# An attention block with Strassen products: v's last sums in place, its transpositions in pieces, and three orders on VectorE

## The chip, the core and the metric

The kernel runs on one core of a Trainium2 chip, as one program. A core has a TensorE (PE, matrix products out of SBUF into PSUM), a VectorE (DVE, element-wise work and transpositions of 32 x 32 blocks), a ScalarE (ACT, the exponential and copies), a GpSimd (POOL) and a SyncE (SP), which here mostly issue DMAs. Each engine takes its instructions in the order of its own queue and waits on semaphores for the others. The metric is the device time of the program in microseconds; lower is better.

## The reference

An input x of 16 images, 512 channels and 32 x 32 points goes through a group norm (8 groups), a product with a 1536 x 512 matrix that gives q, k and v, attention with 4 heads of 128 channels over the 1024 points, a product with a 512 x 512 matrix, and is added to the result. All in float32.

```python
xn = ((xg - mu) * rsqrt(var + EPS)).reshape(b, c, h, w) * gamma + beta
q, k, v = split(einsum('oc,bchw->bohw', qkv_w, xn) + qkv_b, 3, axis=1)   # to heads: b, 4, 1024, 128
attn = softmax(einsum('bhnd,bhmd->bhnm', q, k) * scale, axis=-1)
out = einsum('bhnm,bhmd->bhnd', attn, v)
return x + einsum('oc,bchw->bohw', proj_w, out) + proj_b
```

## The kernel before

**Attention.** The main loop (L2364) takes 16 images x 4 heads x 8 steps of 128 keys. A step has two halves of 512 queries: a product for the scores (`score`, L1704), an exponential on ScalarE into `p` (L1710), and one step later the product with v into `po` (L1801). The running sum `tot` of the exponentials is VectorE's (L1723, L1725). When a head is over, `denominators` transposes it (L1734), sums it and takes the reciprocal; DMAs spread it over the partitions as `rinv`, and `divide` (L1814) multiplies the head's output by it at step 4 of the next head.

**Products between.** Into each half of a step the loop puts one entry of a list `halfway`: a few TensorE units of the products for the next image (q, k, v) or the last one (the projection). So TensorE's order is scores, weighted sum, some units of Strassen products, scores and so on.

**Strassen products.** `strassen` (L623) makes a 2 x 2 block product from seven products p1 to p7, in the order 1, 2, 6, 5, 7, 4, 3, out of weights kept in DRAM and inner sums t1 to t4 of the moving blocks. p1, p6, p7 and p4 gather in a PSUM bank x, p5 and p3 in a bank y, of which there is one (`ps_z`, one buffer). A result c22 is VectorE's sum of bank y and ScalarE's copy of bank x after p7; p3 is written into bank y, so it waits for c22, and c12 is read from y after p3.

**Images 0 to 3** use `two_levels` (L699), a Strassen product of Strassen products: four groups g of inner products, whose results lie in tiles R[0] to R[2] (tags r0 to r2, turned by one from call to call; R[3] is R[0] again). `make_sum` makes the inner sums t1 to t4 of a group on VectorE (L757). `combine` queues the outer sums in `pending`, of which each unit runs one when it is over: `add` (L908) and `done`, which calls the caller's `finish` for the results c11, c22, c21, c12. For v, `finish` (L1056) adds two parts and v's bias into the first half of a tile `vt` of the pool `ypool` (two buffers, tag y), `turn_v` transposes it into the second half of that tile (L1068), GpSimd sends it to DRAM (`vd`, L1076) and reads it back in v's layout (L1087). What is still in `pending` at the end of v's last group goes to a list `late["tail"]`, of which the main loop runs two per half of a step (L2405), behind the step's other units. The products for v of the next image run in head 3, those for q and k of heads 0 and 1 in head 2, those for heads 2 and 3 in head 0 of that image.

**Images 4 to 15** use `thirds` (L1099): 15 outer products in 8 groups for each of two pairs of heads, G = 0 to 15, out of thirds of the columns. They run in heads 2 and 3 of the image before and in head 0, and the last units of G = 15 (p4, p3) in the first half of head 1. `out_` (L1268) evicts their results; L1287 is c22 (and c12) on VectorE. `turn_part` transposes v in 128 x 256 pieces (L1348).

**The projection** of the image before (`proj_groups`, L1645) is a `two_levels` with a `prepare` function and runs in head 1. Its first unit stands in the same half as the last units of the thirds. Its inner sums of group 0 are in the tile home_B, those of group 1 in a tile `pp_t`. The outer sums of its operand (`sums_of_b`, L415) are VectorE's too.

**Order.** A planner lays each engine's instructions in order before the program runs: by priority (by and large the order in which the program names them; `tc.high_priority` puts them ahead) and by when, by its estimate, their inputs are there. `with tc.issue_after(i)` puts the instructions of the block that are on i's engine behind i in that engine's queue. It can place an instruction well ahead of the step that names it. On the chip each queue is then followed as it stands.

Of the kernel before, what the change touches and what calls it, by code (L numbers as in the profile page):

```python
# [16 lines left out]
P = 128  # L17
# [214 lines left out]
def fast_path(ctx, tc, x, sources, out, consts, flag, dims):  # L232
# [466 lines left out]
    def two_levels(name, site, b, blocks, finish, sums="make", homes="BBBB", prepare=None):  # L699
# [11 lines left out]
        def placed():  # L711
            return tc.high_priority(URGENT) if opening else nullcontext()
# [28 lines left out]
        def make_sum(g, m):  # L741
            n = len(OUTER[g])
            to = sum_tile(g, m)
            a, c = {
                "t1": ("b12", "b11"), "t2": ("b22", "t1"), "t3": ("t2", "b11"),
                "t4": ("b21", "t2"),
            }[m]
            with ExitStack() as order:
                if sums == "keep" and g == 0 and m in ("t1", "t2"):


                    order.enter_context(tc.issue_after(added[b - 1, 1, NB - 1].ins))
                    order.enter_context(tc.high_priority(URGENT))
                if (b, site) == (0, 1) and (g > 0 or m in ("t3", "t4")):
                    order.enter_context(tc.issue_after(beside["scores"].ins))
                for i in range(n):
                    nc.vector.tensor_sub(  # L757
                        to[:, i, :], inner_block(g, i, a), inner_block(g, i, c)
                    )
            if sums == "keep":  # L760
                t = dpool.tile([P, n, Q], F32, tag=f"{m}_{g}", bufs=1, name=f"kept_{m}_{g}")
                inner_kept[b, g, m] = t
                nc.gpsimd.dma_start(t, to)

        def group_units(g):
# [99 lines left out]
            def end():  # L865
                combine(g)
                if g == len(OUTER) - 1:
                    if site == "v":
                        late["tail"] = late.get("tail", []) + pending
                    else:  # L870
                        with placed():
                            run(pending)
                    pending.clear()


# [47 lines left out]
        def combine(g):  # L923

            if g == 1 and opening:
# [9 lines left out]

                pending.extend((lambda: None, lower))
            elif g == 1:
                done("c11", (0, 0), (1, 0))
                add((1, 1), (0, 0), (1, 1))
                add((1, 0), (1, 1), (0, 1))  # L940
            elif g == 2 and opening:
                add((2, 0), (1, 1), (2, 0), 0)
# [109 lines left out]
    def v_groups(b):  # L1052
        rows = {}


        def finish(which, h, a, c):  # L1056
            pair, half = int(which[1]) - 1, int(which[2]) - 1
            two = ypool.tile([P, KC, HALF], F32, tag="y", name=f"vt_{b}_{pair}_{h}_{half}")
            t = two[:, 0]
            i = 2 * pair + h  # L1060
            nc.vector.scalar_tensor_tensor(t, a, vb_sb[:, i : i + 1], c, ALU.add, ALU.add)
            turn_v(b, pair, half, h, t, two[:, 1], rows)

        return two_levels(f"v_{b}", "v", b, lambda: xb[b], finish, "load", "ABAB")

    def turn_v(b, pair, half, h, t, u, rows):
        n = P // BLK
        nc.vector.transpose(  # L1068
            u.rearrange("p (q i j) -> p j q i", q=n, i=BLK),
            t.rearrange("p (j q i) -> p j q i", q=n, i=BLK),  # L1070
        )
        if h == 0:
            rows[half] = dpool.tile(
                [2 * P, HALF], F32, tag="v", name=f"vd_{b}_{pair}_{half}"
            )
        nc.gpsimd.dma_start(rows[half][ts(h, P), :], u)  # L1076
        if h == 1:
            read_v(b, pair, half, rows[half])
# [20 lines left out]
    def thirds(b):  # L1099
# [151 lines left out]
        def group_units(G):  # L1251
# [16 lines left out]
            def out_(which, a, c=None):  # L1268
# [14 lines left out]
                with tc.high_priority(URGENT):  # L1283
                    if c is None:
                        evict(dst, view(a), row, G)
                    else:
                        nc.vector.tensor_add(dst, view(a), view(c))  # L1287

            us = strassen(
                f"t_{b}_{G}", mm, out_, n * H3,  # L1290
# [49 lines left out]
        def turn_part(p, h, part):  # L1340
            half, q = divmod(part, 2)
            if (p, half) not in turned:
# [2 lines left out]
                ]  # L1345
            u = turned[p, half][0]
            n = P // BLK
            nc.vector.transpose(  # L1348
                u[:, h].rearrange("p (q i j) -> p j q i", q=n, i=BLK)[:, ds(2 * q, 2)],
                made["vt"][:, h, ts(part, Q)].rearrange("p (j q i) -> p j q i", q=n, i=BLK),  # L1350
            )
            turned[p, half][1] += 1
            if turned[p, half][1] < 2 * KC:
                return
# [374 lines left out]
    def denominators(b, h):  # L1729
# [1 line left out]
        t = tot.pop((b, h))  # L1731

        tt = lpool.tile([P, N // BLK, BLK], F32, tag="tt", name=f"tt_{b}_{h}")
        nc.vector.transpose(tt.rearrange("p c m -> p (c m)"), t)  # L1734
        part = lpool.tile([P, N // BLK], F32, tag="part", name=f"part_{b}_{h}")
        nc.vector.tensor_reduce(part, tt, AX.X, ALU.add)

# [626 lines left out]
    for s in range(steps + 1):  # L2364
# [15 lines left out]
        for half in range(NH2):  # L2380
            if s < steps:
                scores(s, half)
                if j in (2, 3) and half == 0 and s > NB:
                    with tc.issue_after(exps[s].ins):
                        spread_inverse(*where(s - NB)[:2], j - 2)
                if half == 1 and j == 4 and s > NB:

                    with tc.issue_after(added[b, h, 4].ins):
                        divide(*where(s - NB)[:2])
                if half == 1 and s in biased:  # L2390

                    with tc.issue_after(exps[s].ins):
                        bias_of_v(0, biased[s])
# [167 lines left out]
```

## Time and profile before

| | us |
|---|---|
| median of 3 runs | 3120.81 (3120.13 to 3120.99) |
| the profiled execution, its own time | 3120.64 |
| its span, first to last instruction | 3119.1 |
| ScalarE busy | 1727.8 |
| all DMA packets, mean rate | 204 GB/s |

The mean granted TensorE clock is 0.999. A timeline row reads: start in us from the first instruction, length in us, engine, line, operation, tiles written and read, shape, count of merged instructions and, in brackets, the idle time of the engine before it and what ended it. Idle times under 0.15 us aren't printed. A matmul's length has its way through the array in it, so that the next one starts before it ends: a hole is seen in the distance of two starts. A float32 product stands in the records as two matmuls, one behind the other.

In the timeline of TensorE, image 2 begins at 424.8 us, image 4 at 819 us, and from image 4 on each image takes 192.4 us.

### The profile page before, as it was taken

Reading aid. Unit: us, or ns where it says so; the run is one execution under the profiler, and the core shown is the slowest. Engines: PE = TensorE matmul, PEld = TensorE weight load, DVE = VectorE, ACT = ScalarE, POOL = GpSimd, SP = SyncE. Lnnn points to the kernel's source line nnn. Section 1 sums busy time; section 2 is a strip of 40 time slices with the busy share of each in tenths; the row PEclk is TensorE's granted clock in tenths of the full one; section 3 lists DMA queues with packets and bytes.
Section 4 is the critical chain, followed back from the end, with each engine's and each line's share of the span. In section 5 each row is a group of like instructions: output and inputs, shape, how many; then the busy total and the mean of one; then the engine's idle time right before and its main releaser. Section 6 shows DMA issues by size and latency. Waiting matters only on the chain. (4 is left out here: it accounts for less than half of the span.)

```text
span 3119.1 us, 38289 instructions
## 1 busy us (share of the span) xinstructions
PE 3105.8 (100%) x11934; PEld 2265.7 (73%) x11934; DVE 2692.3 (86%) x4604; ACT 1727.8 (55%) x3744; POOL 469.0 (15%) x792
## 2 busy tenths in 40 slices
PE   9999999999999999999999999999999999999999
PEld 7567766777777777777777777777777777777775
DVE  9988888789798897988979889798898988989787
ACT  3545536455465655656556565565655656556543
POOL 0131121111111111211112111111111111111010
PEclk9999999999999999999999999999999999999999
DMA  5576765666767667666676666766667676676651
GB/s 173 173 229 198 246 196 196 211 197 212 233 219 221 194 206 224 199 217 201 200 224 208 215 200 205 222 204 210 204 203 226 198 213 206 211 221 194 222 192 42
DMA packets 244064, 636.80 MB, mean 204 GB/s; under 512 B 32656, under 2 KB 77840, under 8 KB 243856
## 3 DMA queue, kind: packets, MB, share of 16 engines
q1 hardware_dynamic: 164912, 363.58, 38.3%
q0 software_dynamic: 66272, 236.38, 21.8%
q10 hardware_dynamic: 12672, 34.35, 3.5%
q8 instruction: 96, 1.57, 0.2%
q14 instruction: 112, 0.92, 0.1%
HBM read 462.49 MB, written 171.69 MB: 203 GB/s over the span
## 5 line engine op out<-in xcount | busy, mean ns | idle before, releaser
L1801 PE MATMUL po<-p,v 128*128 128x512 f32 x2048 | 1046.3, 593 | 0.0
L1704 PE MATMUL s<-qk,qk 128*128 128x512 f32 x2048 | 1045.6, 592 | 0.0
L1710 ACT ACTIVATE p<-s 128x512 f32<-128x512 f32 x1024 | 610.7, 596 | 520.2 <-PE s L1704 510.6
L1801 PEld LDWEIGHTS po<-p,v 128*128 128x128 f32 x2048 | 616.2, 301 | 375.9 <-issue 259.7
L1725 DVE TENSOR_TENSOR tot<-tot,p 128x1024 f32<-128x1024 f32 (+1 forms) x408 | 472.6, 1159 | 159.8 <-ACT p L1710 156.5
L1704 PEld LDWEIGHTS s<-qk,qk 128*128 128x128 f32 x2048 | 362.0, 189 | 52.3 <-issue 24.2
L1287 DVE TENSOR_TENSOR r<-t_y,t_u 128x342 f32<-128x342 f32 (+1 forms) x384 | 186.4, 485 | 138.6 <-PE t_y L1263 111.6
L1378 DVE TENSOR_TENSOR r<-r,r 128x684 f32<-128x684 f32 x264 | 226.4, 865 | 1.4
L1263 PE MATMUL t_x<-home_A,w 128*128 128x171 f32 x1008 | 187.8, 308 | 0.3 <-DVE home_A L1181 0.3
L1263 PE MATMUL t_x<-home_B,w 128*128 128x171 f32 x1008 | 187.7, 308 | 0.0
L1263 PEld LDWEIGHTS t_x<-home_A,w 128*128 128x128 f32 x1008 | 161.6, 189 | 30.8 <-issue 20.1
L1263 PEld LDWEIGHTS t_x<-home_B,w 128*128 128x128 f32 x1008 | 161.6, 189 | 30.2 <-issue 20.1
L1087 POOL DMA_DIRECT2D v<-vd x240 | 139.7, 589 | 156.5 <-DMA vd<-vu 54.3
L1150 DVE TENSOR_TENSOR f<-x 128x684 f32<-128x684 f32 x168 | 144.1, 858 | 0.8
L1223 ACT COPY t_u<-t_x 128x342 f32<-128x342 f32 x192 | 78.5, 409 | 119.6 <-PE t_x L1263 111.9
L293 POOL DMA_DIRECT2D x<-in_x x60 | 32.7, 548 | 645.2 <-PE t_x L1263 410.4
L1263 PEld LDWEIGHTS t_z<-f,w 128*128 128x128 f32 x528 | 89.5, 190 | 51.9 <-issue 34.4
L792 PE MATMUL pp_x<-home_B,w_proj 128*128 128x256 f32 x414 | 107.1, 379 | 0.0
L1348 DVE STREAM_TRANSPOSE vu<-vt 128x256 f32<-128x256 f32 x192 | 104.7, 647 | 0.0
L1229 ACT ACTIVATE t_u<-t_x,bias 128x171 f32<-128x171 f32 x192 | 72.1, 402 | 56.7 <-PE t_x L1263 56.6
L1263 PE MATMUL t_y<-f,w 128*128 128x171 f32 x528 | 101.3, 310 | 1.3 <-DVE r L1287 0.6
L1188 POOL DMA_DIRECT2D kept_t<-home_A x96 | 52.4, 546 | 321.5 <-DVE home_A L1181 312.1
(393 smaller groups left out, 5227.9 us busy)
## 6 DMA issues: line engine op xcount, KB each, us to landing
w<-kept SPq DMA_DIRECT2D x182, 512.0 KB, 3.9
w<-kept SPq DMA_DIRECT2D x182, 384.0 KB, 3.9
kept_t<-home_A POOLq DMA_DIRECT2D x96, 342.0 KB, 3.8
home_B<-kept_t SPq DMA_DIRECT2D x96, 342.0 KB, 3.3
rinv<-row ACTq DMA_DIRECT2D x63, 512.0 KB, 4.3
x<-in_x POOLq DMA_DIRECT2D x60, 512.0 KB, 5.7
v<-vd POOLq DMA_DIRECT2D x240, 128.0 KB, 4.3
out_y<-y_c POOLq DMA_DIRECT2D x60, 512.0 KB, 3.3
```

Of the source, the lines that this page charges most:

```text
L792: latest["product"] = nc.tensor.matmul(acc[:, ts(i, Q)], have["w"][t][:, i, slot, :], inner(i, bn), start=(first and i == 0), stop=True, s ...
L1087: nc.gpsimd.dma_start(vs[b, pair][ts(q, BLK), half].rearrange("m h (k i) j -> m (h k) (i j)", k=n), rows.rearrange("(k m) (q e) -> q m k e ...
L1150: (eng.tensor_add if op == "+" else eng.tensor_sub)(made[f], of(a), of(c))
L1223: nc.scalar.copy(dst, src)
L1263: latest["product"] = nc.tensor.matmul(acc[:, ts(i, H3)], wts[G, t][:, i, slot, :], moving, start=(start and i == 0), stop=True, skip_grou ...
L1287: nc.vector.tensor_add(dst, view(a), view(c))
L1348: nc.vector.transpose(u[:, h].rearrange("p (q i j) -> p j q i", q=n, i=BLK)[:, ds(2 * q, 2)], made["vt"][:, h, ts(part, Q)].rearrange("p ( ...
L1378: (nc.vector.tensor_add if add else nc.vector.tensor_sub)(at(o), a, c)
L1704: latest["score"] = nc.tensor.matmul(sc, ks[b, h][:, ts(j, P)], qs[b, h][:, ts(half, HALF)], start=True, stop=True)
L1710: exps[s] = nc.scalar.activation(ps[s][:, ts(half, HALF)], sc, AF.Exp, scale=SCALE)
L1725: added[b, h, j] = nc.vector.tensor_add(tot[b, h][:, i], tot[b, h][:, i], ps[s][:, i])
L1801: summed = nc.tensor.matmul(po[half], v_block(b, h, j), ps[s][:, i], start=(j == 0), stop=(j == NB - 1),)
```

## The change

- v's `finish` writes its sum over one of the two parts it adds (over c for c22, else over a), and takes one tile of the pool `ypool` for both heads of a result, for the transposed halves alone. Because c11's sum now overwrites R[0][:, 0], `combine` puts the addition that reads it ahead of c11's two sums when the site is v.
- At the end of v's last group what is left in `pending` is run there, as for the other sites, and not put into `late["tail"]`.
- `turn_v` and `turn_part` transpose in pieces of 128 columns: four instructions in place of one of 512, two in place of one of 256.
- In `thirds`, `late["third"]` holds the latest c22 eviction. The projection's inner sums of group 0, and t3 and t4 of group 1, are put behind it on VectorE, and so is the transposition of `tot` of each head 0.
- In head 0 of image 4 (`old`) `divide` comes at step 5, behind that step's running sum, and not at step 4.

```diff
@@ make_sum
+                if prepare and (g == 0 or (g, m) in ((1, "t3"), (1, "t4"))) and "third" in late:
+                    order.enter_context(tc.issue_after(late["third"].ins))
@@ end
                 if g == len(OUTER) - 1:
-                    if site == "v":
-                        late["tail"] = late.get("tail", []) + pending
-                    else:
-                        with placed():
-                            run(pending)
+                    with placed():
+                        run(pending)
                     pending.clear()
@@ combine
             elif g == 1:
+                if site == "v":
+                    add((1, 1), (0, 0), (1, 1))
                 done("c11", (0, 0), (1, 0))
-                add((1, 1), (0, 0), (1, 1))
+                if site != "v":
+                    add((1, 1), (0, 0), (1, 1))
                 add((1, 0), (1, 1), (0, 1))
@@ v_groups, finish
-            two = ypool.tile([P, KC, HALF], F32, tag="y", name=f"vt_{b}_{pair}_{h}_{half}")
-            t = two[:, 0]
+            if h == 0:
+                rows["to"] = ypool.tile(
+                    [P, KC, HALF], F32, tag="y", name=f"vt_{b}_{pair}_{half}"
+                )
+            t = c if which == "c22" else a
             i = 2 * pair + h
             nc.vector.scalar_tensor_tensor(t, a, vb_sb[:, i : i + 1], c, ALU.add, ALU.add)
-            turn_v(b, pair, half, h, t, two[:, 1], rows)
+            turn_v(b, pair, half, h, t, rows["to"][:, h], rows)
@@ turn_v
-        nc.vector.transpose(
-            u.rearrange("p (q i j) -> p j q i", q=n, i=BLK),
-            t.rearrange("p (j q i) -> p j q i", q=n, i=BLK),
-        )
+        to = u.rearrange("p (q i j) -> p j q i", q=n, i=BLK)
+        of = t.rearrange("p (j q i) -> p j q i", q=n, i=BLK)
+        for k in range(HALF // P):
+            nc.vector.transpose(to[:, k], of[:, k])
@@ thirds, out_
-                        nc.vector.tensor_add(dst, view(a), view(c))
+                        out = nc.vector.tensor_add(dst, view(a), view(c))
+                        if which == "c22":
+                            late["third"] = out
@@ turn_part
-            nc.vector.transpose(
-                u[:, h].rearrange("p (q i j) -> p j q i", q=n, i=BLK)[:, ds(2 * q, 2)],
-                made["vt"][:, h, ts(part, Q)].rearrange("p (j q i) -> p j q i", q=n, i=BLK),
-            )
+            to = u[:, h].rearrange("p (q i j) -> p j q i", q=n, i=BLK)[:, ds(2 * q, 2)]
+            of = made["vt"][:, h, ts(part, Q)].rearrange("p (j q i) -> p j q i", q=n, i=BLK)
+            for k in range(2):
+                nc.vector.transpose(to[:, k], of[:, k])
@@ denominators
-        nc.vector.transpose(tt.rearrange("p c m -> p (c m)"), t)
+        third = late.get("third") if h == 0 else None
+        with tc.issue_after(third.ins) if third is not None else nullcontext():
+            nc.vector.transpose(tt.rearrange("p c m -> p (c m)"), t)
@@ main loop
-                if half == 1 and j == 4 and s > NB:
+                if half == 1 and j == (5 if (b, h) == (old, 0) else 4) and s > NB:
-                    with tc.issue_after(added[b, h, 4].ins):
+                    with tc.issue_after(added[b, h, j].ins):
                         divide(*where(s - NB)[:2])
```

## The prediction

> **What bounds the kernel now.** I read the page first: its span and busy times.
>
> ```profile
> span 3119.1 us, 38289 instructions
> PE 3105.8 (100%) x11934; PEld 2265.7 (73%) x11934; DVE 2692.3 (86%) x4604; ACT 1727.8 (55%) x3744; POOL 469.0 (15%) x792
> ```
>
> TensorE is busy all the time but 13.3 us (3119.1 - 3105.8). The change neither adds nor removes a product, so it can only win what lies in the holes of PE, and in matmuls that run at a lower clock behind a hole. I therefore read PE's timeline around its holes and, in the same places, VectorE's. A group of four 171-column matmuls that follows another without a wait takes 0.59 us from start to start here (1059.67 to 1060.26); that is the measure for holes too short for the view to print.
>
> First hole, in image 2, head 0 (timeline of PE; the bracket is idle time and what ended it):
>
> ```profile
> 437.29 0.59 PE L792 MATMUL qk_x<-xt,w 128*128 128x256 f32 x2
> 440.84 1.13 PE L792 MATMUL qk_y<-x,w 128*128 128x256 f32 x4 [2.95 <-DVE qk_r L830]
> ```
>
> Product p3 (out to bank y) can't begin before VectorE has read c22 out of that bank. The stages behind it (columns: PE, PEld, DVE, ACT, POOL busy, granted clock, DMA share, GB/s) show a second price:
>
> ```profile
> 437.90:440.84 2.94, 0.00 (x0) 0.00 (x1) 2.87 (x8) 0.57 (x1) 1.17 (x2) 1.00 0.27 107
> 440.84:446.00 5.16, 5.16 (x12) 3.06 (x13) 1.77 (x2) 0.60 (x1) 2.63 (x5) 0.67 0.97 277
> ...
> 638.60:644.00 5.40, 5.38 (x19) 3.99 (x20) 1.79 (x2) 1.77 (x3) 2.55 (x5) 1.00 0.67 221
> ```
>
> After the hole the granted clock is 0.67 for 5.16 us: 0.33 x 5.16 = 1.70 us lost. The last row follows the same hole one image later, which is only 1.25 us long; there the clock stays 1.00. So a hole of 2.95 us costs 4.65 us, one of 1.25 us costs itself.
>
> The other holes, image 3 head 0, image 4 head 0, image 4 at the start of head 1:
>
> ```profile
> 638.62 1.13 PE L792 MATMUL qk_y<-x,w 128*128 128x256 f32 x4 [1.25 <-DVE qk_r L830]
> ```
>
> ```profile
> 854.03 0.85 PE L1263 MATMUL t_y<-x,w 128*128 128x171 f32 x4 [1.40 <-DVE r L1287]
> ```
>
> ```profile
> 870.96 0.85 PE L1263 MATMUL t_y<-f,w 128*128 128x171 f32 x4 [0.55 <-DVE r L1287]
> ```
>
> The last of these comes again in each of images 5 to 15, shorter; the first and the last of the eleven:
>
> ```profile
> 1059.67 0.75 PE L1263 MATMUL t_y<-home_B,w 128*128 128x171 f32 x4
> 1060.26 0.74 PE L1263 MATMUL t_x<-home_B,w 128*128 128x171 f32 x4
> ...
> 1062.55 0.75 PE L1263 MATMUL t_x<-home_B,w 128*128 128x171 f32 x4
> 1063.38 0.85 PE L1263 MATMUL t_y<-f,w 128*128 128x171 f32 x4
> 1064.06 1.03 PE L792 MATMUL pp_x<-o,w_proj 128*128 128x256 f32 x4
> ```
>
> ```profile
> 2986.66 0.75 PE L1263 MATMUL t_x<-home_B,w 128*128 128x171 f32 x4
> 2987.46 0.85 PE L1263 MATMUL t_y<-f,w 128*128 128x171 f32 x4
> ```
>
> In image 5 the steps are 0.83 and 0.68 us where 0.59 would do: 0.24 + 0.09 = 0.33 us. In image 15 the first step is 0.80, so 0.21. The restart adds about 0.1 us each time. Everything that the change can reach is then 4.65 + 1.25 + 1.40 + 0.55 + four restarts of 0.1 + eleven times 0.32 = 11.8 us, 0.38% of the run.
>
> **The change, part by part.**
>
> *Ties at the second head.* Before p3 of the last group of thirds stands VectorE's c22 (L1287). VectorE in image 5, and ScalarE's copy that c22 needs:
>
> ```profile
> 1058.09 2.12 DVE L1348 STREAM_TRANSPOSE vu<-vt 128x256 f32<-128x256 f32 x4
> 1060.00 0.46 DVE L757 TENSOR_TENSOR pp_t<-home_A,pp_t 128x256 f32<-128x256 f32 x1
> ...
> 1060.65 1.25 DVE L1725 TENSOR_TENSOR tot<-tot,p 128x1024 f32<-128x1024 f32 x1
> 1061.78 0.78 DVE L757 TENSOR_TENSOR home_B<-o 128x256 f32<-128x256 f32 x2
> ...
> 1062.78 0.55 DVE L1287 TENSOR_TENSOR r<-t_y,t_u 128x342 f32<-128x342 f32 x1
> ```
>
> ```profile
> 1061.04 0.70 ACT L1229 ACTIVATE t_u<-t_x,bias 128x171 f32<-128x171 f32 x2 [0.71 <-PE t_x L1263]
> ```
>
> The copy ends at 1061.74, but three of the projection's inner sums (L757, from 1061.78 to 1062.78, 1.00 us) go first. The tie puts all sums of group 0 behind c22, and t3 and t4 of group 1 (such as the one at 1060.00) with them. c22 then starts at about 1061.8 instead of 1062.78 and ends at 1062.35; p3 could start at 1062.55 + 0.59 = 1063.14. The hole goes, with 0.8 us to spare: 0.33 us in image 5, 11 x 0.32 = 3.5 us in all. In image 4 the same move is worth 0.55 + 0.1 = 0.65 us. What now queues behind c22 are those sums, eight of about 0.4 us; the first that PE needs (t2) is read here:
>
> ```profile
> 1067.51 1.03 PE L792 MATMUL pp_x<-home_B,w_proj 128*128 128x256 f32 x4
> ```
>
> With t1 and t2 done by about 1063.8 there are 3.7 us of cover; without it each microsecond of lateness would be a microsecond of PE, twelve times. The tie of the denominators' transposition alters nothing by itself: it already runs behind that c22, and costs nothing. Bounds of this part: -4.2 us, and 0 if other VectorE work takes the freed place. I take -4.1.
>
> *The division one step later*, in image 4 only:
>
> ```profile
> 852.33 1.22 DVE L1814 TENSOR_TENSOR o<-o,rinv 128x1024 f32<-128x1024 f32 x1
> 853.47 0.51 DVE L1287 TENSOR_TENSOR r<-t_y,t_u 128x342 f32<-128x342 f32 x1
> ```
>
> Without it c22 starts 1.14 us earlier, and 1.40 shrinks to about 0.26. The division's readers are the sums of o for the projection that starts with head 1, where the 0.55 us hole stands, 17 us on. Bounds -1.5 and 0; I take -1.1.
>
> *v's last sums* (images 1 to 3). VectorE in image 2 from the third result of v (c21) on:
>
> ```profile
> 422.69 1.41 DVE L1061 SCALAR_TENSOR_TENSOR vt<-v_r,vb_sb 128x512 f32<-128x512 f32 x2 [1.48 <-DMA vd<-vt]
> 424.02 2.03 DVE L1068 STREAM_TRANSPOSE vt<-vt 128x512 f32<-128x512 f32 x2
> 425.90 0.41 DVE L830 TENSOR_TENSOR v_r<-v_y,v_u 128x256 f32<-128x256 f32 x1
> ...
> 433.08 1.42 DVE L1061 SCALAR_TENSOR_TENSOR vt<-v_r,vb_sb,v_r 128x512 f32<-128x512 f32 x2
> 434.40 2.06 DVE L1068 STREAM_TRANSPOSE vt<-vt 128x512 f32<-128x512 f32 x2
> ...
> 440.10 0.68 DVE L830 TENSOR_TENSOR qk_r<-qk_y,qk_u 128x512 f32<-128x512 f32 x1
> ```
>
> VectorE stands still for 1.48 us because c21's sum has no free "y" buffer until an earlier store lands. Summed in place it needs none, and the transpositions take four buffers of y in place of eight. From 422.69 to 440.10 there is no printed gap. Moving c12's sums and transpositions (433.08 to 436.5) ahead in that full queue therefore doesn't bring c22 forward by their 3.4 us: the same work still stands before it. Only the 1.48 us does. The hole shrinks from 2.95 to 1.47 us, near the 1.25 us after which the clock stayed up, so the 1.70 goes too: -3.2 us. If c12's 3.4 us do free c22, the whole 4.65 goes; if the wait merely moves to the transposition's buffer, nothing. I take -3.2, and nothing for image 3: its queue has no such wait, and there too the sums only change places (bounds -1.35 and 0). Image 1 has little to spare:
>
> ```profile
> 242.29 0.67 DVE L830 TENSOR_TENSOR qk_r<-qk_y,qk_u 128x512 f32<-128x512 f32 x1
> ```
>
> ```profile
> 243.15 1.03 PE L792 MATMUL qk_y<-x,w 128*128 128x256 f32 x4
> ```
>
> c22 ends at 242.96, 0.19 us before PE needs it: cost 0 as long as VectorE isn't later there. In place, a result tile is held until its transposition ends. The first such tile to be written again (c21's) is freed at 425.90 and taken by the next head's first copy:
>
> ```profile
> 430.22 0.58 ACT L838 COPY qk_r<-qk_z 128x512 f32<-128x512 f32 x1 [0.32 <-PE qk_z L792]
> ```
>
> That is 4.3 us of cover. The swap of c11's sums with one addition makes them 1.2 us later; their readers are DMAs for the next head. GpSimd's queue gets the same stores, no more.
>
> *Transpositions in pieces of 128.* From the rows above, 512 columns take 0.94 us start to start ((425.90 - 424.02)/2) and 256 take 0.48 ((1060.00 - 1058.09)/4): proportional, with a fixed part of 0.02 us. No piece of 128 is in the trace. The nearest rows are sums of that width, and the durations of today's transpositions (shortest, median, longest, in ns):
>
> ```profile
> 850.46 0.29 DVE L1572 TENSOR_TENSOR w<-w,w 128x128 f32<-128x128 f32 x1
> 850.67 0.28 DVE L1573 TENSOR_TENSOR w<-w 128x128 f32<-128x128 f32 x1
> 850.99 0.29 DVE L1574 TENSOR_TENSOR w<-w 128x128 f32<-128x128 f32 x1
> ```
>
> ```profile
> L1068 DVE STREAM_TRANSPOSE vt<-vt x24: 1054/1111/1185, 208.8 to 633.5; 128x512 f32<-128x512 f32 x24
> ```
>
> ```profile
> L1348 DVE STREAM_TRANSPOSE vu<-vt x192: 578/644/698, 757.7 to 2983.8; 128x256 f32<-128x256 f32 x192
> ```
>
> A sum that needs nothing of its predecessor starts 0.21 us after it, one that does 0.32. Bounds for a piece: 0.21 (a gain of 0.10 in 512 columns) and, if each waits until the one before it has ended, 0.41 (the medians carried on to 128: 644 - 467/2). I take 0.24, a quarter of 0.94, because the proportional pair is the same instruction: so nothing, and for the 192 of the thirds nothing either.
>
> **Sum.** 4.1 + 1.1 + 3.2 = 8.4 us. The profiled execution took 3120.64 us (span 3119.1 and 1.5 around it), the median of the runs is 3120.81; 3120.6 - 8.4 = 3112.2, and the same holds for the median.
>
> **The rivals.**
>
> 1. *The v heads are freed wholly*: c22 no longer stands behind c12's 3.4 us in images 2 and 3. For it: the queue's order isn't fixed by the program alone. Against it: no gap in that queue. 1.45 and 1.35 us more: 3109.4.
>
> 2. *Each piece pays a fixed part.* Sums do: tot's 1024 columns take 1.13 us (1060.65 to 1061.78) and 128 take 0.21, which leaves 0.08 at no columns. If a transposition has that too, 512 columns grow by three times 0.08, 0.24 us. Six stand before c22 in images 1 and 3, four behind image 2's wait: 1.44 - 0.19, 1.44 and 0.96, together 3.65 us: 3115.9. Against it: the 0.02 of the proportional pair. [...]
>
> 3. *The ties don't do what they say*: other ready work of VectorE takes the place of the sums before c22, and the v heads are as they were. Only the division's 1.1 us remains: 3119.5.
>
> 4. *Slower: the pieces wait for each other*, since they write interleaved places of one tile. At 0.41 us a piece 512 columns take 1.64, 0.70 more. Six stand before c22 in a v head: 4.2 us. Image 3's hole becomes 5.5 us and gets the slow clock (4.2 + 1.7 = 5.9), image 1 gets one (4.2 - 0.2 + 1.7 = 5.7), image 2 loses 4 x 0.70 - 1.48 = 1.3. In the thirds eight pieces are 1.4 us late, which the 0.8 us to spare plus the 0.65 us of sums moved away just covers. 12.9 - 5.2 = 7.7: 3128.3. At 0.32 us a piece this is about zero; it is slower from some 0.40 on. For it: VectorE is 86% busy and full in these places. Against it: today's transpositions overlap, 0.48 apart while each lasts 0.64.
>
> **How the numbers follow.** Forecast 0.46 (own range 3110.5 to 3114.5), rival 1 0.13, rival 2 0.18, rival 3 0.10, rival 4 0.13. What a measurement can tell from no change is 0.2%, 6.2 us. Below 3114.6 lie the forecast and rival 1: faster 0.59. Rivals 2 and 3 are the same: 0.28. Rival 4: slower 0.13. The range 3106.5 to 3120.0 holds the first four and leaves out rival 4 and some of the edges.
>
> **What would show it.** In the changed profile: c22 (L1287's successor) directly behind tot at each second head's start, and steps of 0.59 us on PE there; the hole in image 4 head 0 near 0.3 us; c21's sums in image 2 with no DMA wait, a hole there of 1.5 us and a clock of 1.00 after it; image 3's hole still near 1.25; pieces 0.24 us apart. Pieces over 0.32 apart, a new hole in image 1, or sums of the projection that PE waits for would make it wrong.

## The result, and the profile after

| | before | after |
|---|---|---|
| median | 3119.73 us (3118.61 to 3120.99, 8 runs) | 3110.18 us (3109.36 to 3110.76, 8 runs) |
| span of the profiled execution | 3119.1 us | 3108.6 us |

The ratio is 0.9969, with a 95% interval of 0.9958 to 0.998: about 0.3% faster. The busy times on the page of the changed kernel:

```profile
span 3108.6 us, 38584 instructions
PE 3101.1 (100%) x11934; PEld 2265.5 (73%) x11934; DVE 2691.9 (87%) x4868; ACT 1727.1 (56%) x3744; POOL 468.9 (15%) x792
```

The matmuls are the same 11934, and VectorE's busy time is the same within 0.4 us (2692.3 before), though it has 264 instructions more. So nothing became cheaper. What changed is when things run, and it is to be looked for in the holes of PE again.

**Image 2, head 0.** PE's timeline at the former hole of 2.95 us, and the stage behind it (columns as in the prediction):

```profile
436.62 0.59 PE L794 MATMUL qk_x<-x,w 128*128 128x256 f32 x2
437.05 0.59 PE L794 MATMUL qk_x<-xt,w 128*128 128x256 f32 x2
437.53 0.70 PE L794 MATMUL qk_y<-x,w 128*128 128x256 f32 x2
```

```profile
437.53:442.53 5.00, 5.00 (x19) 3.73 (x19) 2.39 (x5) 2.14 (x4) 0.42 (x1) 1.00 1.01 242
```

The last two starts are 0.48 us apart, the first two 0.43: the hole has gone, and with it the slow stretch (clock 1.00). VectorE shows why, at c21 and at c22:

```profile
419.78 1.41 DVE L1066 SCALAR_TENSOR_TENSOR v_r<-v_r,vb_sb 128x512 f32<-128x512 f32 x2
421.10 1.57 DVE L1076 STREAM_TRANSPOSE vt<-v_r 128x128 f32<-128x128 f32 x6
...
436.86 0.62 DVE L832 TENSOR_TENSOR qk_r<-qk_y,qk_u 128x512 f32<-128x512 f32 x1
437.40 0.17 DVE L1768 SCALAR_TENSOR_TENSOR worst<-l,r 32x32 f32<-32x32 f32 x1
437.51 0.07 DVE L1768 DVE_READ_ACCUMULATOR worst<-l,r 32x1 f32 x1
437.51 0.67 DVE L415 TENSOR_TENSOR home_A<-home_A,o 128x512 f32<-128x512 f32 x1
```

c21's sums have no wait in brackets any more (1.48 us before). And c22 (L832) has moved ahead of the third sum of o (L415) and of `worst`. In the kernel before both stood ahead of it (c22 began at 440.10 us there):

```profile
438.06 0.18 DVE L1759 SCALAR_TENSOR_TENSOR worst<-l,r 32x32 f32<-32x32 f32 x1
...
439.50 0.68 DVE L415 TENSOR_TENSOR home_A<-home_A,o 128x512 f32<-128x512 f32 x1
```

From start to start these are 0.12 + 0.60 us, which the prediction did not have. c12's sums and transpositions still run ahead of c22.

**Image 3 and image 4**, the two holes of head 0, and the start of image 4's head 1:

```profile
632.63 1.13 PE L794 MATMUL qk_y<-x,w 128*128 128x256 f32 x4 [0.27 <-DVE qk_r L832]
```

```profile
847.69 0.85 PE L1268 MATMUL t_y<-x,w 128*128 128x171 f32 x4 [0.87 <-DVE r L1292]
...
863.33 0.75 PE L1268 MATMUL t_x<-home_B,w 128*128 128x171 f32 x4
864.10 0.85 PE L1268 MATMUL t_y<-f,w 128*128 128x171 f32 x4
```

1.25 became 0.27, 1.40 became 0.87, and 0.55 became a step of 0.77 instead of 0.59 (0.18). VectorE before image 4's c22:

```profile
844.32 0.29 DVE L1578 TENSOR_TENSOR w<-w 128x128 f32<-128x128 f32 x1 [2.33 <-DMA w<-in_qkv_wT]
...
845.39 1.22 DVE L1732 TENSOR_TENSOR tot<-tot,p 128x1024 f32<-128x1024 f32 x1
846.52 0.68 DVE L415 TENSOR_TENSOR home_A<-o,o 128x512 f32<-128x512 f32 x1
847.13 0.51 DVE L1292 TENSOR_TENSOR r<-t_y,t_u 128x342 f32<-128x342 f32 x1
```

The division is gone from there, but a sum of o (0.61 us from start to start) has taken half of its place, and the longest wait ahead of this c22 is as long as it was: 2.33 us for weights (2.32 before).

**Images 5 to 15**, the second heads: PE, then VectorE, in image 5.

```profile
1055.70 0.75 PE L1268 MATMUL t_x<-home_B,w 128*128 128x171 f32 x4
1056.29 0.74 PE L1268 MATMUL t_y<-f,w 128*128 128x171 f32 x4
1056.87 1.03 PE L794 MATMUL pp_x<-o,w_proj 128*128 128x256 f32 x4
```

```profile
1053.47 1.23 DVE L1732 TENSOR_TENSOR tot<-tot,p 128x1024 f32<-128x1024 f32 x1
1054.91 0.51 DVE L1292 TENSOR_TENSOR r<-t_y,t_u 128x342 f32<-128x342 f32 x1 [0.21 <-ACT t_u L1234]
```

Steps of 0.59 and 0.58. c22 stands directly behind tot, waits 0.21 us for ScalarE's copy and ends at 1055.42, 0.87 us before its product. The same holds in all eleven images.

Summed as excess of PE's start-to-start distances over what a step takes without a wait (for image 2 and images 5 to 15 with the restart of 0.1 us: the same product takes 0.85 us behind the hole at 1063.38 before and 0.74 without one at 1056.29 after), in us:

| place | before | after | won |
|---|---|---|---|
| image 2, hole and restart | 3.22 | 0.15 | 3.1 |
| image 2, slow stretch | 1.65 | 0 | 1.65 |
| image 3, head 0 | 1.41 | 0.44 | 1.0 |
| image 4, head 0 | 1.56 | 1.03 | 0.5 |
| image 4, start of head 1 | 0.72 | 0.19 | 0.5 |
| images 5 to 15, eleven times | 0.34 | 0 | 3.7 |
| everywhere else | | | 0.1 |
| all | 26.7 | 16.1 | 10.55 |

### The profile page after: what moved, and what is told of

Its sections match the earlier page's. It is cut to its first block, busy times and chain, and to the rows that moved or that the text cites. A ratio compares the mean times of both kernels' runs of the same rounds, so it can differ in the third digit from the quotient of the medians.

```text
span 3108.6 us, 38584 instructions
## 1 busy us (share of the span) xinstructions
PE 3101.1 (100%) x11934; PEld 2265.5 (73%) x11934; DVE 2691.9 (87%) x4868; ACT 1727.1 (56%) x3744; POOL 468.9 (15%) x792
## 4 chain that ended last, share of the span: by engine, by line
PE 97%; DVE 1%; issue 1%; DMA 0%; POOL 0%; POOLq 0%; DVEq 0%
PE s L1711 28%; PE po L1810 28%; PE t_x L1268 13%; PE t_y L1268 7%; PE pp_x L794 6%; PE t_z L1268 3%; PE qk_x L794 3%; PE pp_y L794 3%; PE qk_y L794 2%; PE pp_z L794 1%; PE v_x L794 1%; PE qk_z L794 1%; PE v_y L794 1%; PE v_x L1027 0%; PE v_z L794 0%
## 5 line engine op out<-in xcount | busy, mean ns | idle before, releaser
L1358 DVE STREAM_TRANSPOSE vu<-vt 128x128 f32<-128x128 f32 x384 | 106.2, 401 | 0.0
L1363 POOL DMA_DIRECT2D vd<-vu x48 | 34.8, 726 | 436.4 <-DVE vu L1358 436.4
```

Of the source, the lines that this page charges most:

```text
L1358: nc.vector.transpose(to[:, k], of[:, k])
```

## The experiments

Where a kernel was timed in rounds, its ratio is to the kernel before on the same chip. "Hole" is the excess of the table above. The first four make one part of the change each. The diffs are excerpts.

**e1: the ties alone** (`out_` keeps the latest c22 as in the change).

```diff
 make_sum
+                if prepare and (g == 0 or (g, m) in ((1, "t3"), (1, "t4"))) and "third" in late:
+                    order.enter_context(tc.issue_after(late["third"].ins))
 denominators
+        third = late.get("third") if h == 0 else None
+        with tc.issue_after(third.ins) if third is not None else nullcontext():
```

> The kernel before with the two ties behind the thirds' c22 and nothing else. Theory: they alone remove the short holes at the start of the second heads. TensorE's steps there are 0.58 to 0.59 us in images 5 to 15 (0.83 and 0.68 before), the hole of image 4 shrinks from 0.55 to about 0.1, the holes in images 2, 3 and 4 head 0 stay at 2.95, 1.25 and 1.40: 4.1 us less than before. Rival: the holes went because pieces and v's new places shifted VectorE's queue; then the steps stay near 0.8 and the time is within 1 us of before.

3116.11 us (3115.26 to 3117.35) against 3120.19 us, ratio 0.9987 [0.9977, 0.9997]. The eleven holes of images 5 to 15 are gone (3.7 us); the one at the start of image 4's head 1 is not (0.74, before 0.72): the sums of home_B no longer stand ahead of c22 there, but two sums into pp_t (L759, 0.66 us from 868.11 on) have taken their place. Image 2's hole is as long as before, and yet:

```profile
440.76 1.13 PE L794 MATMUL qk_y<-x,w 128*128 128x256 f32 x4 [2.95 <-DVE qk_r L832]
```

```profile
440.76:445.76 5.00, 5.00 (x18) 3.73 (x19) 1.77 (x2) 1.57 (x3) 2.16 (x4) 1.00 0.92 250
```

The clock behind the same 2.95 us is 1.00 here and 0.67 in the profile of before. So between these two profiled executions 1.65 us of the difference are not the ties' doing.

**e2: v's part whole** (sums in place and the run at the end of the group, with the tile of `ypool` for both heads and the order for c11 as in the change), transpositions whole, no ties.

```diff
 end
-                    if site == "v":
-                        late["tail"] = late.get("tail", []) + pending
-                    else:
-                        with placed():
-                            run(pending)
+                    with placed():
+                        run(pending)
 finish
-            two = ypool.tile([P, KC, HALF], F32, tag="y", name=f"vt_{b}_{pair}_{h}_{half}")
-            t = two[:, 0]
+            t = c if which == "c22" else a
```

> The kernel before with v's sums in place and run at the end of v's last group, transpositions whole, no ties. Theory as predicted: only the 1.48 us wait for a buffer goes; image 2's hole shrinks from 2.95 to 1.5, the clock behind it is 1.00, image 3's stays at 1.25: 3.2 us less. Rival: the new order of VectorE's queue also puts work behind image 2's c22, and back-to-back dependent operations are spread; then image 2's hole is under 0.5 and image 3's under 0.7: 5 to 6 us less.

3116.6 us (3115.58 to 3117.1), ratio 0.9989 [0.9979, 0.9999]. Image 2's hole is 1.32 us with no slow stretch, image 3's 0.75. Images 5 to 15 keep theirs. Image 4's head 0 shows 0.82: its wait for weights was 1.58 us here, 2.32 before.

**e3: the pieces alone.**

```diff
 turn_v (and the same in turn_part, two pieces)
-        nc.vector.transpose(u.rearrange(...), t.rearrange(...))
+        for k in range(HALF // P):
+            nc.vector.transpose(to[:, k], of[:, k])
```

> The kernel before with all of v's transpositions in pieces of 128 and nothing else. Theory: 0.23 to 0.24 us a piece, so no gain and no loss; holes of images 2 and 3 within 0.3 us of 2.95 and 1.25, time within 1 us of before. Rival: the pieces themselves let c22 through between them or are cheaper in the full queue; then image 2's hole falls under 2 us and the slow clock goes, 2 us or more less.

3115.16 us (3114.21 to 3118.08), ratio 0.9986 [0.9976, 0.9995]: the part forecast at nothing is alone worth as much as the others. Not by its own time, but by the order that it gives VectorE. In image 2:

```profile
439.22 0.67 DVE L830 TENSOR_TENSOR qk_r<-qk_y,qk_u 128x512 f32<-128x512 f32 x1
439.81 0.17 DVE L1759 SCALAR_TENSOR_TENSOR worst<-l,r 32x32 f32<-32x32 f32 x1
439.92 0.07 DVE L1759 DVE_READ_ACCUMULATOR worst<-l,r 32x1 f32 x1
439.92 0.67 DVE L415 TENSOR_TENSOR home_A<-home_A,o 128x512 f32<-128x512 f32 x1
```

c22 stands ahead of `worst` and the last sum of o; image 2's hole is 2.17 us and has no slow stretch. At the second heads one inner sum of the projection that ran between the transpositions and tot in the kernel before (pp_t, 0.32 us) now runs later:

```profile
1056.10 2.06 DVE L1351 STREAM_TRANSPOSE vu<-vt 128x128 f32<-128x128 f32 x8
1058.02 0.40 DVE L757 TENSOR_TENSOR pp_t<-home_A,pp_t 128x256 f32<-128x256 f32 x1
1058.35 1.19 DVE L1725 TENSOR_TENSOR tot<-tot,p 128x1024 f32<-128x1024 f32 x1
```

That covers the 0.24 us by which c22 was late, and all eleven holes of images 5 to 15 are gone without a tie. Eight pieces take 1.92 us here (1056.10 to 1058.02); four pieces of 256 took 1.91 before.

**e4: the division one step later, alone** (behind `added[b, h, j]`, as in the change).

```diff
-                if half == 1 and j == 4 and s > NB:
+                if half == 1 and j == (5 if (b, h) == (old, 0) else 4) and s > NB:
```

> The kernel before with the division of image 4's head 0 one step later and nothing else. Theory as predicted: c22 1.14 us earlier, the hole shrinks from 1.40 to 0.26, 1.1 us less. Rival: one of the o sums (L415, 0.6 us a start) moves into the place of the division; then the hole is 0.8 to 0.9 and 0.5 us are won.

3120.25 us (3118.87 to 3121.88), ratio 1.0 [0.999, 1.001]. The hole in image 4's head 0 is what it was, 1.56 us: L415 is in the division's place, and the wait for weights was 2.86 us. The one at the start of head 1 shrank from 0.72 to 0.20: the queue there has c22 between the transpositions now, not behind all of them. A hole of 0.23 us came up later in that head, and the second heads of images 5 to 15 have their holes as before, two of them (images 5 and 10) 0.2 us longer.

**e5: the changed kernel with whole transpositions.** Its edit is e3's, undone.

> The changed kernel with whole transpositions again (512 and 256 columns). Theory: a piece costs its share (0.232 us start to start for 128 against 0.94 for 512), but four short instructions instead of a long one let the planner place other work between them; in the v heads that order is worth about 1.3 us in image 2 and 0.3 us in image 3, as the holes of e2 (1.32, 0.75) stand against those of the changed kernel (0.04, 0.44). In the thirds the ties alone hold the order, so images 5 to 15 have no hole. Time 3110.2 + 1.6 = 3111.8 us (3111 to 3113). Rival 1: the pieces do nothing beside the rest: 3110.2 (within 0.5 us). Rival 2: they carry alone what they gave when made alone (e3: 4.6 us): 3114.8.

3112.03 us (3111.3 to 3112.83), ratio 0.9972 [0.9962, 0.9982]; 1.85 us above the changed kernel's median, which was taken in another series. Image 2's hole is 1.31 us, image 3's 0.74, images 5 to 15 have none above 0.2 us. VectorE before image 2's c22:

```profile
436.75 0.69 DVE L415 TENSOR_TENSOR ot<-o,home_A 128x512 f32<-128x512 f32 x1
437.36 0.68 DVE L415 TENSOR_TENSOR home_A<-home_A,o 128x512 f32<-128x512 f32 x1
437.96 0.68 DVE L832 TENSOR_TENSOR qk_r<-qk_y,qk_u 128x512 f32<-128x512 f32 x1
```

All three sums of o are ahead of c22 again. So in the changed kernel the pieces are worth 1.3 us in image 2 and 0.3 us in image 3, through the order; in the second heads the ties do the same alone. In image 4's head 0 it is the other way round: the hole is 0.50 us here and 1.03 in the changed kernel, with a wait for weights of 1.84 us against 2.33.

**e6: v's sums in place, alone**; **e7: the run at the end of the group, alone.** The edits are the two halves of e2's diff (e6 with the addition for c11 put ahead, as in the change).

> The kernel before with v's sums in place alone; what is left of v's last group still runs in the next head, transpositions are whole, no ties, divide at step 4. Theory: the place takes away VectorE's wait for a buffer (1.48 us in image 2) and nothing else, so image 2's hole is 1.5 to 1.7 us, image 3's 1.3 to 1.5, image 5's steps still 0.83 and 0.68. Rival: the run at the end of the group is what shortens the hole in e2; then image 2 still shows about 3.0 us here.

> The kernel before with what is left of v's last group run at its end alone; sums not in place, transpositions whole, no ties. Theory: without the place the buffer wait stays or grows (the last sums ask for a buffer sooner), so image 2's hole is 2.5 us or more; in image 3, which has no such wait, the hole goes from 1.41 to about 0.75 as in e2. Rival: the run at the end does it, and image 2's hole is about 1.3 us as in e2, image 3's 1.4.

e6: 3117.2 us in one run. e7: 3121.49 us. VectorE at c21's sums, then PE at c22's reader, first of e6, then of e7:

```profile
420.26 1.41 DVE L1067 SCALAR_TENSOR_TENSOR v_r<-v_r,vb_sb 128x512 f32<-128x512 f32 x2
```

```profile
438.93 0.48 PE L792 MATMUL qk_y<-x,w 128*128 128x256 f32 x1 [1.16 <-DVE qk_r L830]
```

```profile
423.03 1.41 DVE L1058 SCALAR_TENSOR_TENSOR vt<-v_r,vb_sb 128x512 f32<-128x512 f32 x2 [2.02 <-DMA vd<-vt]
```

```profile
441.16 1.13 PE L792 MATMUL qk_y<-x,w 128*128 128x256 f32 x4 [3.45 <-DVE qk_r L830]
```

With the place alone the wait is gone and PE idles 1.16 us, as in e2; with the run alone the wait grows to 2.02 us and PE's idle time to 3.45. In image 3 the hole is 0.83 us in e6 and 1.42 in e7. So what e2 wins in images 2 and 3 is the place; the run at the end alone wins nothing in either image. Both expectations had image 3 the wrong way round: it was the place there too.

**e8: pieces of 64.**

```diff
         for k in range(HALF // P):
-            nc.vector.transpose(to[:, k], of[:, k])
+            for r in range(2):
+                nc.vector.transpose(to[:, k, ts(r, 2)], of[:, k, ts(r, 2)])
```

> The changed kernel with transpositions in pieces of 64 columns. Theory: the time is proportional to the columns, so a piece of 64 stands 0.116 to 0.13 us behind the last (0.232 / 2 and up). Rival: a fixed part of about 0.08 us, as the sums have, shows at this width at the latest: 0.16 us or more, which is 0.7 us more in 512 columns and 4 us more before image 3's c22.

3109.34 us in one run. The groups of transpositions by form (shortest, median and longest in ns), first after, then e8, and a row of e8's timeline with its successor:

```profile
L1076 DVE STREAM_TRANSPOSE vt<-v_r x96: 365/389/425, 211.0 to 622.1; 128x128 f32<-128x128 f32 x96
```

```profile
L1077 DVE STREAM_TRANSPOSE vt<-v_r x192: 253/273/327, 211.0 to 622.1; 128x64 f32<-128x64 f32 x192
```

```profile
405.60 2.19 DVE L1077 STREAM_TRANSPOSE vt<-v_r 128x64 f32<-128x64 f32 x16
407.65 1.20 DVE L907 TENSOR_TENSOR v_r<-v_r,v_r 128x1024 f32<-128x1024 f32 x1
```

Sixteen pieces take 2.05 us from start to start, 0.128 each. With 0.94 for 512 columns, 0.48 for 256 and 0.23 for 128 the fixed part is 0.01 to 0.02 us a piece, not 0.08. Halving again doesn't cost what the rival says, and gives still finer places for other work: image 2's c22 stands at 435.94, 0.9 us earlier than after, and image 3's hole is gone. Image 4's is 1.48 us; its wait for weights was 2.64.

**e9: o's sums behind c22** in images 2, 3 and 4; **e10: and the weights of G = 14 too.** Both stand on the changed kernel.

```diff
 e9, at the call of sums_of_b
-                plan[6].append(lambda: sums_of_b(ob[b - 1]))
+                if b in (2, 3):
+                    plan[6].append(lambda: behind(late["first"], lambda: sums_of_b(ob[b - 1])))
+                elif b == old:
+                    plan[6].append(lambda: behind(late["sixth"], lambda: sums_of_b(ob[b - 1])))
 e10, in sum_weights
-                inner_weights(w, size(G))
+                with tc.issue_after(late["sixth"].ins) if (
+                    G == 2 * count - 2 and "sixth" in late
+                ) else nullcontext():
+                    inner_weights(w, size(G))
```

`late["first"]` is c22 of the first group of q and k for heads 2 and 3, whose products run in head 0, `late["sixth"]` that of G = 13.

> The changed kernel with the sums of o for the projection (L415) put behind c22: in images 2 and 3 behind that of the first group of heads 0 and 1, in image 4 behind that of G = 13. Theory: what is left of the holes is VectorE's order, so image 3's hole (0.44 us) goes, and image 4's (1.03) shrinks by the one L415 that stands ahead of its c22 (0.60) to about 0.4. Time 3110.2 - 1.0 = 3109.2 us. Rival: the sums of o are late for the projection, which costs what is won: a new hole at the projection's first units in head 1 and 3110.2 or more.

> e9, and with it the four sums of the weights of G = 14 (each waiting, through the first, for a DMA of 2.3 us) put behind G = 13's c22 too. Theory: the hole in image 4 is tot and c22 behind weights that the queue has no need of yet; it goes altogether: 1.03 us and the restart of 0.1 against the changed kernel, 0.44 and 0.1 from image 3. Time 3108.5 us (3107.8 to 3109.5), a little faster than the changed kernel. Rival: c22 is late for another reason (ScalarE's copy, the running sum), and the hole stays at 0.4 us or more: 3109.2. A second rival: G = 14's products now wait for their weights, 0.5 us or more: 3110.

e9: 3109.22 us in one run; image 3's hole is gone, image 4's is 0.36. A hole of 1.1 us came up 12 us later in e9, where PE waits for the sums of the weights of G = 15. e10: 3107.81 us (3107.69 to 3108.32, 5 runs), ratio 0.9958 [0.9944, 0.9972]; that is 2.4 us under the changed kernel's median of another series, whose fastest run (3109.36) is slower than the slowest here. VectorE, then PE, in image 4:

```profile
843.65 0.51 DVE L1297 TENSOR_TENSOR r<-t_y,t_u 128x342 f32<-128x342 f32 x1 [0.65 <-ACT t_u L1233]
844.08 0.28 DVE L1585 TENSOR_TENSOR w<-w 128x128 f32<-128x128 f32 x1
```

```profile
845.27 0.45 PE L1273 MATMUL t_x<-f,w 128*128 128x171 f32 x2
845.56 0.74 PE L1273 MATMUL t_y<-x,w 128*128 128x171 f32 x4
```

c22 waits for ScalarE's copy alone, and the weights' sums behind it don't wait at all: their transfer has landed by then. PE's step is 0.29 us for two matmuls, without a hole, and G = 14's products start without one too. No hole over 0.25 us is left in images 1 to 15.

**e11 and e12: holes made on purpose**, to see when the clock drops. In images 5 to 15 VectorE makes sums that nobody reads ahead of the c22 of G = 15.

```diff
 e11, out_
+                            for _ in range(b - old + 1):
+                                last = nc.vector.tensor_add(
+                                    spare[:, : n * H3], c[:, : n * H3], c[:, : n * H3]
+                                )
 e12, the same with (5, 6, 7, 8, 8, 9, 9, 9, 10, 10, 11)[b - old - 1] sums, and in the main loop
+            held = s < steps and b > old and h == 1 and 0 < 2 * j + half < 6
+            after_p3 = tc.issue_after(late["p3"].ins) if held else nullcontext()
+            after_p3.__enter__()
```

> The changed kernel with 2, 3, ... 12 sums of 342 columns, which nobody reads, ahead of the c22 of G = 15 in images 5, 6, ... 15. Each takes about 0.4 us on VectorE; with 0.8 us to spare PE's hole there grows from 0 to about 4 us. Theory: the slow stretch belongs to the length of the hole, by chance between about 2.9 and 3.4 us (2.95 and 2.91 us had it in the kernel before and e4, 2.95 had not in e1, 3.45 had in e7) and never below 2.1: so granted clock 1.00 behind all holes under 2.1 us, below 0.9 behind the last ones over 3.4 us, each of these costing some 1.5 us beside itself. Rival: it belongs to the place (a head's first step, DMAs at their full rate), so the clock stays 1.00 behind every hole here.

> As e11, but what TensorE does after p3 of G = 15 in images 5 to 15 (the projection's later units, scores and weighted sums of the next three halves) is put behind p3, so that the planner can't fill the hole with it; 5, 6, 7, 8, 8, 9, 9, 9, 10, 10 and 11 added sums in images 5 to 15, 0.545 us each (e11: 6.57 us for twelve). One product of the projection (0.86 us) stands ahead of p3, so the holes are about 0.545 n - 1.7: 1.0, 1.5, 2.1, 2.6, 2.6, 3.2, 3.2, 3.2, 3.7, 3.7, 4.3 us. Theory: the slow stretch belongs to the length of the hole: granted clock 1.00 behind the first three, below 0.9 behind the last three, by chance between; each slow stretch costs about 1.6 us. Time 3110.2 + 31 + 5 x 1.6 = 3149 us. Rival: it belongs to the place (the first step of an image, its DMAs at full rate), and the clock is 1.00 behind all eleven: 3141 us.

e11 missed its aim: 3114.53 us, and no hole there over 0.52 us. The planner counted the sums too and put the projection's products, scores and weighted sums ahead of p3. e12 holds these behind: 3147.99 us. The table has the idle time before p3 from PE's timeline, and the clock of the stage of 5 us behind each hole; four of these stages:

```profile
2030.09:2035.09 5.00, 5.00 (x13) 2.82 (x14) 5.00 (x12) 2.29 (x4) 4.24 (x7) 0.66 0.91 242
2227.12:2232.12 5.00, 5.00 (x19) 3.71 (x20) 5.00 (x12) 3.17 (x6) 4.24 (x7) 1.00 0.96 221
...
2817.62:2822.62 5.00, 5.00 (x19) 3.71 (x20) 5.00 (x12) 3.17 (x6) 4.11 (x7) 1.00 0.92 243
3014.06:3019.06 5.00, 5.00 (x13) 3.42 (x14) 5.00 (x12) 1.19 (x2) 4.73 (x8) 0.68 0.88 247
```

| image | 5 | 6 | 7 | 8 | 9 | 10 | 11 | 12 | 13 | 14 | 15 |
|---|---|---|---|---|---|---|---|---|---|---|---|
| idle before p3, us | 0.80 | 1.35 | 1.90 | 2.45 | 2.45 | 3.00 | 3.00 | 3.00 | 3.55 | 3.54 | 4.10 |
| clock behind it | 1.00 | 1.00 | 1.00 | 1.00 | 1.00 | 0.66 | 1.00 | 0.66 | 0.66 | 1.00 | 0.68 |

The place isn't it: four of six holes of 3 us or more have the slow stretch in a second head too. No hole up to 2.45 us has it, and above that the length alone doesn't tell: 3.00 us has it twice and goes without once, and 3.54 goes without. What does tell is worked out in the last section. "Below 0.9 behind the last three" was a miss by one.

## Why the prediction was right, point by point

The forecast was 3112.2 us and 8.4 us won. Won were 9.55 us by the medians and 10.5 between the profiled executions. The forecast's own range ended at 3110.5, so the result stands between it and rival 1 (3109.4). The holes of images 2 and 3 did shrink by nearly what rival 1 gives them, but not for its reason: c12's sums and transpositions still stand ahead of c22. That the sum came so near is in part luck: two terms came out too large (image 4's two holes, and the slow stretch, which was counted whole) and two too small (image 2's and image 3's holes).

**The ties, -4.1.** Right in the mechanism, and -3.7 in size. c22 is directly behind tot, the steps are 0.59, and e1 shows that the ties do it alone. The part that failed is image 4's 0.65: e1 leaves that hole at 0.74, and e4 takes it down to 0.20. The prediction put the division's effect on the hole behind it and none on this one, 17 us on; it was the other way round.

**The division, -1.1.** Wrong in its place. The prediction took the row in front of c22 and counted its time as won. But the planner filled the place with a sum of o (L415), and the queue behind depends on a transfer of weights, whose wait moved from 1.58 us (e2) to 2.86 us (e4) between kernels that don't touch it. In the changed kernel 0.5 us was won there; e4 alone won nothing there. That the weights and the sums of o were the cause is shown by e10, which moves just these and closes the hole.

**v's sums, -3.2: the wait of 1.48 us and the slow stretch.** Right, and short by 1.6. The statement that moving c12's 3.4 us ahead does nothing for c22 is borne out by e6: there c12's sums run 6.2 us earlier, and the hole shrinks by 1.79 us, to 1.33: the wait of 1.48 and 0.3 of small gaps. It is the place that does it; by e7 the run at the end does nothing. The other 1.3 us are the pieces' (e5).

**Image 3: nothing.** Wrong by 1.0. e6 gives 0.6 of it, and no single wait explains that. From v's second result (c22) on to the c22 that PE waits for, VectorE's idle times sum to 0.33 us in the kernel before, 0.13 of it ahead of c21's sums, and to 0.15 in e6; and one inner sum of the next product (L757, 0.33 us) fewer stands in that stretch, five in place of six. Those two make 0.5 us; the rest is open. The pieces give 0.3 more (e5).

**The pieces, nothing.** The price was right: 0.24 was taken, 0.232 was measured (median from start to start in v's transpositions), and rivals 2 (0.08 us of fixed part) and 4 (0.41 us a piece) fall with e8. In these transpositions 0.94, 0.48, 0.23 and 0.128 us for 512, 256, 128 and 64 columns are proportional but for 0.02. But "so nothing" is the step that failed. Shorter instructions give the planner finer places, and that moved c22 ahead of two others in image 2 (e3, e5). The working went from an instruction's time to the kernel's time and left out the order.

**The slow stretch, -1.70.** Its size holds: 0.34 x 5.00 = 1.70 in e12. Its condition, a hole's length between 1.25 and 2.95 us, was taken from two holes and fails: of the ten holes of 2.91 to 4.10 us in the profiles of all kernels here, seven had it (before, e4, e7, and four in e12) and three had not. Nor does every execution have it. In all 14 profiles the granted clock of the whole run is 0.999 or less just where there is a slow stretch, and 1.000 elsewhere. Of the 31 executions of the kernel before that were timed beside e1 to e4, 17 had 0.999 and 14 had 1.000, with medians of 3120.89 and 3119.30 us. All eight of the changed kernel had 1.000. So the change removes a loss of 1.6 us that about half of the executions had, and the forecast counted it in all of them. That fits the 10.5 us between two profiles, one with it and one without, and the 9.55 between medians. Four of e3's ten executions had 0.999 as well (median 3116.34 us, the others 3114.66), though the hole of its profiled execution is 2.17 us long and went without.

**The parts don't add up.** The medians of e1 to e4 are 4.1, 3.6, 5.0 and -0.1 us below before: 12.6, where all together gave 9.55. Executions at a granted clock of 1.000 alone, against the 3119.30 us of the kernel before, give 3.9, 2.7, 4.6 and 0.0: 11.2. The ties and the pieces close the same eleven holes, so 3.7 us stand twice in both sums. The other way round, image 2's hole shrinks by 1.8 us in e2 and by 0.95 in e3, and by 3.1 with both.

## What to carry to other kernels

Where a planner lays the queues, cost an edit by what it lets move, not by its own time alone: look at what stands in the queue ahead of the instruction that ends the hole, and ask of each whether it has to. The best of these kernels came from that question alone (e10: two more orders, 2.4 us), and the row to begin with was the longest bracket in front of the late instruction, 2.33 us for a transfer that c22 had no need of. And a part that is taken out or made alone can be worth more than its share in the whole: two that close the same hole are counted twice.

## What the runs showed of the hardware

By the length of the hole, the clock's drop looks like chance: the kernel before and e1 had the same 2.95 us and differed (0.67 and 1.00), and e12 has three holes of 3.00 us of which one went free, and one of 3.54. Read in finer stretches, the traces show more. The slow stretch is 3.41 us at half the clock (0.50), and it begins 1.35 us after the hole's end in the kernel before. The times between two changes of the clock are whole multiples of 3.4133 us in the trace of the kernel before (436.91, 3.41 and 2672.64 us: 128, 1 and 783 of them) and in that of the changed kernel (3102.72 us: 909), as if the clock could change only on a grid. Two steps of that grid in the kernel before, and one in e12, at the hole of 3.00 us that went free:

```profile
438.78:442.19 3.41, 1.35 (x5) 1.06 (x6) 3.28 (x6) 0.00 (x0) 2.52 (x5) 1.00 0.33 103
442.19:445.60 3.41, 3.41 (x6) 1.68 (x5) 0.51 (x1) 0.60 (x1) 1.28 (x2) 0.50 0.97 287
```

```profile
2225.40:2228.81 3.41, 1.69 (x7) 1.33 (x8) 3.34 (x10) 0.00 (x0) 3.28 (x6) 1.00 0.59 149
```

PE was idle for 2.06 us of the step ahead of the slow one (3.41 - 1.35). The hole of 3.00 us in e12 lies across two steps, with 1.27 us in one and 1.72 in the other (3.41 - 1.69). Counted so, between the kernel's first microseconds and its end, each of the seven slow steps follows a step with 2.06 to 3.41 us of idle PE: 2.06 in the kernel before, 2.4 in e4, by estimate from the lengths of its products 2.1 in e7, and, with e12's grid carried on from the step shown, 2.66, 2.50, 2.11 and 3.41 in its images 10, 12, 13 and 15. At e12's other seven holes no step has more than 1.88 us, and none is followed by a slow one. So by these traces it is not the hole's length that decides but how much of it falls into one step, with the limit somewhere between 1.88 and 2.06 us; where the grid lies against the program differs from execution to execution (the first stretch at the full clock begins 5.28 us after the first instruction in the kernel before and 5.89 in the changed kernel), and by these traces that is the chance in it. It fits that e3's hole of about 2 us cost some executions the clock and others not, but no trace shows these executions. The loss is steady: half the clock for 3.41 us, 1.70 us, in the kernel before, and 0.34 x 5.00 = 1.70 us behind three holes of e12.
